# First convolution of 14 images by 2x2 minimal filtering: 16 products of 256 columns in place of 18 matmuls of 512

## The chip, the core and the metric

The kernel runs on one core of a Trainium2 chip. TensorE (PE) does matmuls into PSUM, VectorE (DVE) and ScalarE (ACT) do elementwise work, and the engines run beside each other, each through its own queue in order. The metric is the device time of one execution in microseconds, as a median of several.

## The reference, cut to what matters

Attention over 16 images of 128 channels and 32 x 32 pixels (4 heads, 1024 positions), then two 3x3 convolutions on quantised data:

```python
x = attention(x)                     # 4 heads, softmax over 1024 keys, residual
out = act_quant(x)                   # 16 levels: integers 0..15
out = conv3x3(out, weight_quant(w1)) # integers -7..7
out = batchnorm(out); out = act_quant(out)
out = conv3x3(out, weight_quant(w2))
out = batchnorm(out) + x
```

Activations and weights of the first convolution are small integers, so bf16 products summed in fp32 are exact.

## The kernel before

Attention is spread over steps: each head has 8 steps of one score group (`pss`, two fp32 matmuls, four records in the trace), one exponential on ScalarE (`e`) and one group of products with the values (`psa`). Other work is placed at fixed steps between them and shares two PSUM buffers, the pool `ps_m`: projections of queries (`psu`) and values (`psv`), and the first convolution of the image before.

```python
vp  = pool("vo", NCH + 4)            # NCH = 8: 12 value tiles
smp = pool("small", 4)
ps_m = pool("ps_m", 2, space=PSUM)
...
def project_v(b, j):
    ps = ps_m.tile([P, NH * P], F32, tag="mm", ...)
    nc.tensor.matmul(ps, lhsT=xt[b][:, ts(j, P)], rhs=bt_sb..., ...)
    vos[b, j] = vp.tile([P, NH * P], F32, tag="vo", ...)
    nc.vector.tensor_copy(vos[b, j], ps)
...
def conv(pool, tag, b, n, r, rows=RPH, group=None):
    ps = pool.tile([P, rows, W], F32, tag=tag, ...)
    for tap in range(NTAP):          # 9 matmuls of 512 columns per half image
        nc.tensor.matmul(ps, lhsT=wq[n][:, tap, :],
                         rhs=pads[b % NPAD][:, r + dy : r + dy + rows, dx : dx + W], ...)
    nc.scalar.copy(ys[b][:, r * W : (r + rows) * W], ps)
...
end = (b + 1) * NH * NCH + 2
at(end + 4, quantize, b, xt, A_LEVELS, 0.0)
for hf in range(NHF):
    at(end + 7 + hf, first_conv, b, hf * RPH)
at(end + 10, statistics, b, 0)
...
if j in (3, 4) and g + 1 < len(heads): project_u(g + 1, j - 3)
if j in (5, 6) and b + 1 < B:          project_v(b + 1, 2 * h + j - 5)
```

A scheduler fixes the order of each engine's instructions when the kernel is built (the static order). It may move work away from the step that asked for it.

## Time and profile before

| | before |
|---|---|
| time | 2154.43 us (median of 3, 2154.38 to 2155.27) |
| PE busy | 98% of the span |
| VectorE / ScalarE busy | 58% / 32% |

A group's line gives its busy time and the mean duration of one instruction. These are rows of the kernel before, each shape on its own (columns: line, engine, operation, out<-in, shapes, count, then busy us and mean ns, then idle before):

```profile
L275 PE MATMUL psc<-pad,wq 128*128 128x512 bf16 x558 | 127.9, 383 | 0.6 <-DVE pad L250 0.6
L283 ACT COPY y<-psc 128x512 f32<-128x512 f32 x62 | 36.2, 584 | 58.1 <-PE psc L275 57.5
```

The mean of 383 ns is a length with the pipeline in it. 558 matmuls in 127.9 us of busy time are 229 ns each. TensorE idled 0.6 us in all before these matmuls.

### The profile page before, as it was taken

What the parts mean: (1) busy time and instruction counts of PE and PEld (TensorE: products, weight loads), DVE (VectorE), ACT (ScalarE), POOL (GpSimd) and SP (SyncE); (2) the same over time, 40 slices, a digit from 0 to 9 for tenths busy, and PEclk for the clock granted to TensorE, in tenths of its full rate; (3) what the DMA queues carried; (4) which work ended last, traced back from release to release, by engine and by line L of the source; (5) the groups of instructions that cost most, each with busy time, mean ns of one, the idle gap of its engine ahead of it and who ended that gap; (6) DMA issues with size and microseconds to landing.
All of it is one profiled execution on the core that took longest, in us unless ns stands there. A gap on an engine that the chain in (4) does not pass through costs nothing.

```text
span 2154.1 us, 14436 instructions
## 1 busy us (share of the span) xinstructions
PE 2118.2 (98%) x5293; PEld 947.3 (44%) x5294; DVE 1256.5 (58%) x1791; ACT 695.3 (32%) x764; POOL 6.8 (0%) x16
## 2 busy tenths in 40 slices
PE   9999999999999999999999999999999999999994
PEld 4444444444444444444444444444444444444541
DVE  3665565556456565556646555665655655665676
ACT  2233232333233333333323323333332333323355
POOL 0000000000000000000000000000000000000000
PEclk9999999999999999999999999999999999999997
DMA  1000000000000000000000000000000000000043
GB/s 60 11 20 0 0 20 0 20 0 10 10 0 20 0 20 0 0 20 0 20 0 20 0 0 20 0 20 0 18 3 0 20 0 10 1 0 10 0 166 157
DMA packets 10606, 36.79 MB, mean 17 GB/s; under 512 B 1440, under 2 KB 1568, under 8 KB 10528
## 3 DMA queue, kind: packets, MB, share of 16 engines
q1 hardware_dynamic: 9872, 33.76, 4.2%
q10 hardware_dynamic: 656, 2.03, 0.3%
q8 instruction: 43, 0.70, 0.1%
q14 instruction: 35, 0.29, 0.0%
HBM read 19.01 MB, written 16.78 MB: 17 GB/s over the span
## 4 chain that ended last, share of the span: by engine, by line
PE 98%; DVE 1%; DMA 0%; ACT 0%; issue 0%; ACTq 0%; DVEq 0%
PE pss L480 41%; PE psa L504 40%; PE psc L275 6%; PE psv L459 5%; PE psu L448 5%; PE psa L619 1%; DVE y L777 1%; DMA wvo_sb<-in_wvo_dram 0%; ACT y L776 0%; DVE late L285 0%; PE ps_b L420 0%; ACT y L283 0%; DVEq L963 0%; PE ps_a L412 0%; ACTq L386 0%
## 5 line engine op out<-in xcount | busy, mean ns | idle before, releaser
L480 PE MATMUL pss<-u,x 128*128 128x512 f32 (+1 forms) x2064 | 962.4, 589 | 0.0
L504 PE MATMUL psa<-e,vo 128*128 128x512 f32 x2016 | 947.6, 592 | 0.0
L493 ACT ACTIVATE e<-pss 128x1024 f32<-128x1024 f32 x511 | 522.9, 1023 | 1305.3 <-PE pss L480 1269.2
L515 DVE TENSOR_TENSOR es<-es,e 128x1024 f32<-128x1024 f32 x378 | 461.3, 1220 | 475.3 <-ACT e L493 471.5
L480 PEld LDWEIGHTS pss<-u,x 128*128 128x128 f32 x2064 | 392.1, 190 | 487.2 <-issue 467.8
L504 PEld LDWEIGHTS psa<-e,vo 128*128 128x128 f32 x2016 | 382.6, 190 | 471.4 <-issue 466.4
L467 DVE COPY vo<-psv 128x512 f32<-128x512 f32 x128 | 88.2, 689 | 259.7 <-PE psv L459 259.7
L275 PE MATMUL psc<-pad,wq 128*128 128x512 bf16 (+3 forms) x585 | 132.0, 380 | 0.6 <-DVE pad L250 0.6
L448 PE MATMUL psu<-x,at_sb 128*128 128x512 f32 x256 | 131.1, 594 | 0.2 <-DVE at_sb L414 0.2
L459 PE MATMUL psv<-bt_sb,x 128*128 128x512 f32 x256 | 130.4, 592 | 0.0
L453 DVE TENSOR_SCALAR u<-psu,au_sb 128x512 f32<-128x512 f32 x64 | 47.9, 749 | 87.2 <-PE psu L448 87.2
L275 PEld LDWEIGHTS <-wq 128*128 128x128 bf16 x585 | 56.7, 97 | 79.9 <-issue 15.3
L527 DVE TRANSPOSE_TENSOR_REDUCE part<-es 128x32 f32<-128x1024 f32 (+1 forms) x66 | 80.6, 1221 | 2.2
L562 DVE STREAM_TRANSPOSE rb<-sums 128x1024 f32<-128x1024 f32 (+1 forms) x66 | 80.1, 1213 | 2.3
L513 DVE TENSOR_TENSOR es<-e,e 128x1024 f32<-128x1024 f32 x63 | 76.6, 1216 | 0.0
L448 PEld LDWEIGHTS psu<-x,at_sb 128*128 128x128 f32 x256 | 48.8, 191 | 61.3 <-issue 60.5
L459 PEld LDWEIGHTS psv<-bt_sb,x 128*128 128x128 f32 x256 | 48.6, 190 | 61.2 <-issue 61.2
L573 DVE TENSOR_TENSOR av<-av,rb 128x1024 f32<-128x1024 f32 x47 | 57.6, 1226 | 3.3
L574 DVE TENSOR_TENSOR acc<-acc,av 128x1024 f32<-128x1024 f32 x47 | 57.4, 1221 | 1.0
L283 ACT COPY y<-psc 128x512 f32<-128x512 f32 (+2 forms) x65 | 37.5, 578 | 59.2 <-PE psc L275 58.7
L520 ACT COPY av<-psa 128x512 f32<-128x512 f32 x63 | 36.9, 586 | 44.6 <-PE psa L504 44.6
L553 DVE COPY side<-part 32x32 f32<-32x32 f32 x252 | 43.0, 171 | 4.7
(98 smaller groups left out, 467.2 us busy)
## 6 DMA issues: line engine op xcount, KB each, us to landing
x_dram<-x SPq DMA_DIRECT2D x16, 512.0 KB, 2.6
res<-x_dram SPq DMA_DIRECT2D x16, 512.0 KB, 9.9
x<-in_x_dram SPq DMA_DIRECT2D x15, 512.0 KB, 3.6
out_dram<-y SPq DMA_DIRECT2D x15, 512.0 KB, 4.7
raw<-in_cw_dram ACTq DMA_DIRECT2D x2, 576.0 KB, 3.7
wvo_sb<-in_wvo_dram ACTq DMA_DIRECT2D x1, 514.0 KB, 7.8
out_dram<-y SPq DMA_DIRECT2D x2, 256.0 KB, 2.0
wqk_sb<-in_wqk_dram SPq DMA_DIRECT2D x1, 385.5 KB, 7.0
```

The source lines that it names most:

```text
L275: last = nc.tensor.matmul(ps, lhsT=wq[n][:, tap, :], rhs=pads[b % NPAD][:, r + dy : r + dy + rows, dx : dx + W], start=(tap == 0), stop=(t ...
L448: nc.tensor.matmul(ps, lhsT=at_sb[:, h, :], rhs=xt[b][:, ts(hf, HALF)], start=True, stop=True)
L459: nc.tensor.matmul(ps, lhsT=xt[b][:, ts(j, P)], rhs=bt_sb.rearrange("p h o -> p (h o)"), start=True, stop=True,)
L467: nc.vector.tensor_copy(vos[b, j], ps)
L480: last = nc.tensor.matmul(ps[:, ts(m, N // len(parts))], lhsT=xt[b][:, ts(key, P)], rhs=us[g][:, queries], start=True, stop=True,)
L493: exps[:] = [nc.scalar.activation(e, ps, AF.Exp).ins]
L504: nc.tensor.matmul(psa[g][m], lhsT=vos[b, j][:, ts(h, P)], rhs=e[:, ts(m, HALF)], start=(j == 0), stop=(j == NCH - 1),)
L513: nc.vector.tensor_tensor(es[g], es.pop((g, 0)), es.pop((g, 1)), ALU.add)
L515: added = nc.vector.tensor_tensor(es[g], es[g], es.pop((g, j)), ALU.add)
L527: nc.vector.tensor_reduce(part, total.rearrange("p (k c) -> p k c", c=Q), AX.X, ALU.add, apply_transpose=True,)
L562: nc.vector.transpose(rb, rinv.unsqueeze(2).to_broadcast([P, n, Q]))
L573: nc.vector.tensor_tensor(av, av, rb, ALU.mult)
```

## The change

It computes the first convolution of images 0 to 13 in 2x2 output tiles. A 4x4 piece of input is transformed (differences and sums of rows, then of columns), multiplied by transformed weights in 16 places, and the 16 results are added and subtracted into four outputs. Instead of 18 matmuls of 512 columns there are 16 of 256. The values stay exact: half and quarter integers in bf16. The transforms go to VectorE, which has room on average.

```diff
+        def transform_rows(b, part):       # 4 ops of 544 elements per image, bf16
+                nc.vector.tensor_tensor(rows[b][:, k], pick(x), pick(y), op)
+        def transform_columns(b, l):       # 4 ops of 1024, operands with step 2
+            nc.vector.tensor_tensor(tiles[b][:, l % 2], pick(x), pick(y), op)
+        def products(b, l):
+            m = qtp.tile([P, 4, D, D], F32, tag="qt", ...)
+            for k in (0, 2):
+                ps = ps_m.tile([P, 2, D, D], F32, tag="mm", ...)
+                for i in range(2):
+                    nc.tensor.matmul(ps[:, i], lhsT=wino[:, l, k + i, :],
+                                     rhs=tiles[b][:, l % 2, k + i], start=True, stop=True)
+                nc.scalar.copy(m[:, k : k + 2], ps)
+            nc.vector.tensor_tensor(e, m[:, 0:2], m[:, 2:3].to_broadcast(...), ALU.add)
+            nc.vector.tensor_tensor(into[0], e[:, 0], m[:, 3], ALU.add)
+            nc.vector.tensor_tensor(into[1], e[:, 1], m[:, 3], ALU.subtract)
+            if l >= 2: ...                 # two more ops of 512 into y
...
-                for hf in range(NHF):
-                    at(end + 7 + hf, first_conv, b, hf * RPH)
-                at(end + 10, statistics, b, 0)
+                for i in range(2):
+                    at(end + 5 + i, transform_rows, b, i)
+                    at(end + 7 + i, transform_columns, b, i)
+                    at(end + 14 + i, products, b, i)
+                    at(end + 17 + i, transform_columns, b, 2 + i)
+                    at(end + 22 + i, products, b, 2 + i)
+                at(end + 26, statistics, b, 0)
```

Cut: the one-time weight transform, and tags that let tiles share memory.

More of the change, by code (lines that the diff above doesn't have):

```diff
@@ L377, in load @@
             nc.sync.dma_start(out=xt[b], in_=x[b])
-        wqk_sb = once.tile([P, NH, 2 * P + 1], F32, name="wqk_sb")
-        wvo_sb = once.tile([P, NH, 2 * P + 1], F32, name="wvo_sb")
+        wqk_sb = once.tile([P, NH, 2 * P + 1], F32, tag="rows", name="wqk_sb")
+        wvo_sb = once.tile([P, NH, 2 * P + 1], F32, tag="tiles", name="wvo_sb")
         xt[0] = xp.tile([P, N], F32, tag="x", name="x0")
@@ L628, in attend_group @@
             if j + 1 == FIRST_STEP[i + 1] and not final:
-                avs[i] = avp.tile([P, HALF], F32, tag="avh", name=f"av_{LAST}_{i}")[:, 0:n]
+                avs[i] = avp.tile([P, N], F32, tag="av", name=f"av_{LAST}_{i}")[:, 0:n]
                 nc.scalar.copy(avs[i], psa[LAST, i])
@@ L658, in fast_path, with sums_and_differences @@
             at((n + 1) * NCH, lambda n: conv_weights(n, once, exps[0]), n)
+        wino = once.tile([P, 4, 4, P], BF16, name="wino")
+        D = W // 2
+        def sums_and_differences(out, src):
+            nc.vector.tensor_copy(out[:, 0], src[:, 0])
+            nc.vector.tensor_copy(out[:, 1], src[:, 2])
+            nc.vector.tensor_tensor(out[:, 3], src[:, 0], src[:, 2], ALU.add)
+            nc.vector.tensor_tensor(out[:, 2], out[:, 3], src[:, 1], ALU.add)
+            nc.vector.tensor_tensor(out[:, 3], out[:, 3], src[:, 1], ALU.subtract)
+            nc.vector.tensor_scalar(out[:, 2:4], out[:, 2:4], 0.5, None, ALU.mult)
@@ new lines, in transform_weights @@
+        def transform_weights():
+            with tc.issue_after(sums_added[0]):
+                by_row = once.tile([P, 4, 3, P], BF16, tag="rows", name="wino_rows")
+                sums_and_differences(by_row, wq[0].rearrange("p (y x) o -> p y x o", x=3))
+                sums_and_differences(wino, by_row.rearrange("p y x o -> p x y o"))
+        rows, tiles = {}, {}
+        OF_FOUR = (
+            (0, 2, ALU.subtract),
+            (3, 1, ALU.subtract),
+            (1, 2, ALU.add),
+            (2, 1, ALU.subtract),
+        )
@@ new lines, in transform_rows @@
+        def transform_rows(b, part):
+            pad = pads[b % NPAD]
+            if part == 0:
+                rows[b] = once.tile([P, 4, D, W + 2], BF16, tag="rows", name=f"rows_{b}")
+            pick = lambda r: pad[:, r : r + 2 * D - 1 : 2, :]
+            for k in (2 * part, 2 * part + 1):
+                x, y, op = OF_FOUR[k]
+                nc.vector.tensor_tensor(rows[b][:, k], pick(x), pick(y), op)
+        def transform_columns(b, l):
+            if l % 2 == 0:
+                tiles[b] = once.tile([P, 2, 4, D, D], BF16, tag="tiles", name=f"tiles_{b}_{l}")
+            pick = lambda c: rows[b][:, :, :, c : c + 2 * D - 1 : 2]
+            x, y, op = OF_FOUR[l]
+            nc.vector.tensor_tensor(tiles[b][:, l % 2], pick(x), pick(y), op)
@@ new lines, in products @@
+        def products(b, l):
+            m = qtp.tile([P, 4, D, D], F32, tag="qt", name=f"wino_{b}_{l}")
+            for k in (0, 2):
+                ps = ps_m.tile([P, 2, D, D], F32, tag="mm", name=f"psw_{b}_{l}_{k}")
+                for i in range(2):
+                    nc.tensor.matmul(
+                        ps[:, i],
+                        lhsT=wino[:, l, k + i, :],
+                        rhs=tiles[b][:, l % 2, k + i],
+                        start=True,
+                        stop=True,
+                    )
+                nc.scalar.copy(m[:, k : k + 2], ps)
+            y = ys[b].rearrange("p (i r j c) -> p r i j c", r=2, j=D, c=2)
+            e = once.tile([P, 2, D, D], F32, tag="raw", name=f"winoe_{b}_{l}")
+            nc.vector.tensor_tensor(
+                e, m[:, 0:2], m[:, 2:3].to_broadcast([P, 2, D, D]), ALU.add
+            )
+            into = [y[:, r, :, :, l] for r in range(2)] if l < 2 else [e[:, r] for r in range(2)]
+            nc.vector.tensor_tensor(into[0], e[:, 0], m[:, 3], ALU.add)
+            nc.vector.tensor_tensor(into[1], e[:, 1], m[:, 3], ALU.subtract)
+            if l >= 2:
+                for c in range(2):
+                    op = ALU.subtract if (l, c) == (3, 1) else ALU.add
+                    nc.vector.tensor_tensor(y[..., c], y[..., c], e, op)
@@ L690, in fast_path @@
         at(NCH + 4, lambda: constants(cleared.ins, sums_added[0]))
+        at(NCH + 6, transform_weights)
         at(2 * NCH + 4, late_bn_constants)
```

## The prediction

> **What bounds the kernel now.** I read the page's busy shares first, then the chain that ended last, then the timeline of two stretches: one with a first convolution, one where the change puts its second pair of product groups.
>
> ```profile
> PE 2118.2 (98%) x5293; PEld 947.3 (44%) x5294; DVE 1256.5 (58%) x1791; ACT 695.3 (32%) x764; POOL 6.8 (0%) x16
> ...
> PE 98%; DVE 1%; DMA 0%; ACT 0%; issue 0%; ACTq 0%; DVEq 0%
> ```
>
> TensorE is busy 98% of the span and the chain is 98% PE. Nothing else ever makes it wait for long, so a microsecond taken from its queue is a microsecond of the end, as long as no new wait appears in that queue. The other engines have room on average: VectorE 58%, ScalarE 32%.
>
> The timeline shows how dense it is, around the first convolution of image 14, whose halves are like those of the 14 images that change:
>
> ```profile
> 1836.69 2.15 PE L275 MATMUL psc<-pad,wq 128*128 128x512 bf16 x9
> ...
> 1838.67 1.88 PE L504 MATMUL psa<-e,vo 128*128 128x512 f32 x4
> ...
> 1840.39 1.88 PE L480 MATMUL pss<-u,x 128*128 128x512 f32 x4
> ```
>
> Starts are what to read (a duration contains the pipeline's length). Nine convolution matmuls take 1838.67 - 1836.69 = 1.98 us, 0.220 each. Four fp32 records take 1.72 us, 0.43 each. So one first convolution costs 2 x 1.98 = 3.96 us of TensorE, and 14 of them 55.4 us, 2.6% of the span.
>
> The price of a 256-column product is in the tail, where one piece of a convolution has 8 rows of 32:
>
> ```profile
> 2052.07 0.58 ACT L283 COPY y<-psc 128x512 f32<-128x512 f32 x1 [1.40 <-PE psc L275]
> ...
> 2053.07 0.37 ACT L283 COPY y<-psc 128x256 f32<-128x256 f32 x1 [0.42 <-PE psc L275]
> ```
>
> Each copy starts when its nine matmuls are done, so nine 256-column ones with their nine weight loads took 2053.07 - 2052.07 = 1.00 us, 0.111 each.
>
> The last stretch is head 3 of an image, from its third score step on. The change wants its second half of products there:
>
> ```profile
> 245.81 1.88 PE L480 MATMUL pss<-u,x 128*128 128x512 f32 x4
> 247.52 1.88 PE L504 MATMUL psa<-e,vo 128*128 128x512 f32 x4
> ```
>
> ```profile
> 246.28 1.22 DVE L574 TENSOR_TENSOR acc<-acc,av 128x1024 f32<-128x1024 f32 x1
> 247.42 0.68 DVE L467 COPY vo<-psv 128x512 f32<-128x512 f32 x1
> 248.02 1.22 DVE L513 TENSOR_TENSOR es<-e,e 128x1024 f32<-128x1024 f32 x1
> 249.34 1.22 DVE L515 TENSOR_TENSOR es<-es,e 128x1024 f32<-128x1024 f32 x1
> 250.48 0.68 DVE L467 COPY vo<-psv 128x512 f32<-128x512 f32 x1
> ```
>
> The two value projections of head 2 ended near 229 and 234, yet VectorE copies them out only at 247.42 and 250.48. They wait because the pool of value tiles (12: eight of this image, four of the next) has no free slot until head 3 has used its first tile, and then VectorE finishes a normalisation. All that time they hold both PSUM buffers of the small pool, the one the products need. In the kernel before nobody asks for these buffers until the projection at 250.96, so the hold is free.
>
> **What the Trainium skill says.** "TensorE: Matmul & The Clock Gate", section "Back-to-back issue gap", gives N/2.4 + 2.5 ns, 109 ns at 256 columns and 216 at 512; the trace has 111 and 220, so it agrees within 2%. The same page, section "The mechanism" of its Part 3, says weight loads overlap matmuls in flight only if they are for other row groups. The trace disagrees: 947.3 us of full-array loads lie under a PE that is 98% busy. "PSUM — Partial Sum Buffer", section "Engine vs sequencer instructions", says matmuls start and complete in program order. The trace agrees (I saw no record out of order), which means that one product that waits holds up everything behind it. "VectorE: DVE Perf Modes", section "What auto-detection actually checks", allows a two-source op its doubled rate only if every operand is 16-bit with step 1. The row transform fits that, the column transform (step 2) does not. The trace before has no bf16 two-source op, so I price all of them at the fp32 rate.
>
> **The change, part by part.**
>
> Removed from TensorE: 18 x 0.220 = 3.96 us per image. Added: 16 x 0.111 = 1.78 us. The operands are contiguous, so this may come out at 0.109. Could the fp32 weight load (190 ns) that follows a 0.11 us product stick out? In the tail's single records, fp32 loads between 8-column matmuls start 0.110 and 0.112 us apart, so it can keep up with a 256-column product; I count nothing. Net gain if nothing waits: 2.18 us per image, 30.5 us in all.
>
> Added to VectorE per image, from fp32 two-source rows (0.42 us for 256 elements, 0.68 for 512, 1.22 for 1024, so by interpolation 0.72 for 544): 4 row ops 2.9, 4 column ops 4.9, 4 sums of 512 2.7, 8 of 256 3.4, 4 into y 2.7: 16.6 us, some 232 us in all, plus about 8 us once for the weights. VectorE goes from 1256 to about 1495 us, 70%. ScalarE makes 8 copies of 0.58 us instead of 2: +3.5 us per image, +49 us. Both lie beside TensorE. The placement decides whether they stay there.
>
> So I followed the new static order of the engines with the durations of the trace. First half (groups l = 0, 1, steps 0 and 1 of head 2): both small PSUM buffers are free. ScalarE copies four pieces between exponentials (step 3.43 us, exponential 1.02, two copies 1.17, av copy 0.59: fits). VectorE's normalisation ends some 3 us later than now, but the copy that frees the attention accumulator stays ahead of the products' sums. Four exponential buffers allow a lag of about three steps; VectorE has caught up two or three steps later. No wait.
>
> Second half (head 3): the order puts the first two products of l = 2 right behind the third score step, and they wait for VectorE. In the trace's times the scores end at 247.52 and the vo copy that frees the buffer ends at 248.10; with the 0.06 us from VectorE to PE seen at the second convolution's start, the product starts at 248.16: PE waits 0.64 us. The next pair, behind one attention step, needs ScalarE's copy of the first, done near 249.4: no wait. The third needs the copy of the second: ready about 251.18, wanted at 251.20. The fourth needs the vo copy that ends at 251.16: in time. So one wait of 0.64 us per image, 9.0 us in all.
>
> Sum: 14 x (3.96 - 1.78 - 0.64) = 14 x 1.54 = 21.6 us; 2154.4 - 21.6 = 2132.8. The order of all three engines from head 60 on is the same in both kernels, so the tail gives nothing and costs nothing. I leave 2133.
>
> **Rivals.**
>
> A: no new wait counts. The full 30.5 us come, 2124. For it: the engines have room on average. Against: the held buffers are in the trace, and the queue is in order.
>
> B: VectorE becomes the local bound. Per head its work is about 18 us of 31, but from step 7 to step 2 of the next head it is nearly full already (a normalisation chain of about 7.5 us and three sums of 1.2 in 10.3 us). If the strided ops cost half again as much as priced, the lag passes from head 2 into head 3, the vo copies come later, and the wait grows to 2 us or more: the gain is gone, 2150 to 2160. Against: I count over 8 us of VectorE idle between the two halves.
>
> C: ScalarE's four copies in a row at head 3. The third and fourth products have a margin of 0.02 to 0.3 us. Copies that start 0.2 us later would cost another 0.1 to 0.4 us per image: 2135 to 2138.
>
> D: switching between fp32 and short bf16 groups (five groups per image) costs about 0.1 us each: 7 us, 2140.
>
> **Range and chances.** The sure part is 30.5 us of matmul time. The least sure is the wait, 0.64 us x 14 by my count; C and D each add up to 7 us, B more. Most errors I can see make it slower than 2133, and A bounds the other side. I take 2123 to 2146. Faster by over 2% needs 2111, which even A doesn't reach: 0.01. Slower by over 2% needs 2198, a wait of 5 us per image: 0.02. Within 2%: 0.97.
>
> **What would show it.** The products' 256-column matmuls should start 0.109 to 0.112 us apart inside a group. PE should show one idle stretch of about 0.6 us in head 3 of each of 14 images, ahead of the first l = 2 product, ended by VectorE's vo copy, 8 to 10 us in all. The period of an image should fall from 127.57 us (convolution to convolution in the chain, as 306.05 to 433.62) to about 126.0. VectorE busy should be 1450 to 1500, ScalarE about 745. I am wrong in the step "one wait" if PE idles elsewhere (before scores, on exponentials or accumulators), and in the step on weight loads if the fp32 matmul behind a group starts more than 0.13 us after the last product.

## The result

The changed kernel took 2132.52 us (median of 4, 2132.12 to 2134.57), against 2154.41 for the kernel before. The ratio is 0.9899, with a 95% interval of 0.9884 to 0.9914. The prediction was 2133.

Busy shares and the last chain of the changed kernel, by engine:

```profile
PE 2089.5 (98%) x5265; PEld 938.9 (44%) x5266; DVE 1445.9 (68%) x2139; ACT 735.7 (35%) x848; POOL 6.8 (0%) x16
...
PE 91%; DVE 7%; ACT 1%; issue 0%; DMA 0%; ACTq 0%; DVEq 0%
```

TensorE is still the bound, but the chain is no longer PE alone: 7% of it runs through VectorE. That is the sign of a wait that is on the path. The view of waits of TensorE says which (columns: who waits, on whom, us in total, times, longest; `psw` is the PSUM tile of the products):

```profile
PE psw L711 <- DVE vo L467: 6.6, 14, 0.5
```

There are 14 waits, one per image, ended by the copy of a value projection. They look smaller than they are, because the view counts from the modelled end of the last matmul. Read from start to start, the product comes 1.06 us after the last score record ahead of it, where 0.43 is usual: 0.63 us late. Summed over the single records that is 8.87 us for the 14. The timeline of TensorE in head 3 of the last changed image shows one of them:

```profile
1878.08 1.88 PE L504 MATMUL psa<-e,vo 128*128 128x512 f32 x4
1879.79 1.88 PE L480 MATMUL pss<-u,x 128*128 128x512 f32 x4
1882.13 0.38 PE L711 MATMUL psw<-tiles,wino 128*128 128x256 bf16 x2 [0.46 <-DVE vo L467]
1882.35 1.88 PE L504 MATMUL psa<-e,vo 128*128 128x512 f32 x4
1884.07 0.38 PE L711 MATMUL psw<-tiles,wino 128*128 128x256 bf16 x2
1884.29 1.02 PE L480 MATMUL pss<-u,x 128*128 128x512 f32 x2
1885.15 0.60 PE L711 MATMUL psw<-tiles,wino 128*128 128x256 bf16 x4
```

and VectorE at the same time:

```profile
1880.26 1.23 DVE L574 TENSOR_TENSOR acc<-acc,av 128x1024 f32<-128x1024 f32 x1
1881.40 0.68 DVE L467 COPY vo<-psv 128x512 f32<-128x512 f32 x1
1882.00 1.22 DVE L513 TENSOR_TENSOR es<-e,e 128x1024 f32<-128x1024 f32 x1
```

The scores free TensorE at 1879.79 + 1.72 = 1881.51, the copy ends at 1881.40 + 0.68 = 1882.08, and the product starts at 1882.13. Every other start follows without a gap. Two products take 0.22 us (1882.13 to 1882.35, 1884.07 to 1884.29), also where fp32 matmuls follow, and the last four begin 0.86 us after the two score records ahead of them, which is just what those take.

The trace shows that two things make this wait. The copy needs a value tile, and the one that it gets comes free when the products of head 3's first step end, at 1878.08 + 1.88 = 1879.96. By then VectorE has reached the end of its normalisation, and the static order puts the add into `acc` (1880.26, 1.23 us) ahead of the copy. Had the copy stood before that add, it would by my estimate have ended near 1880.26 + 0.68 = 1880.94, before the scores free TensorE. So the missing tile alone would not make TensorE wait; the add ahead of the copy does the rest. No run changed that order.

The rows of the new work in the changed kernel:

```profile
L703 DVE TENSOR_TENSOR tiles<-rows 128x1024 bf16<-128x1024 bf16 x56 | 67.1, 1219 | 0.5
L718 ACT COPY wino<-psw 128x512 f32<-128x512 f32 x112 | 61.3, 589 | 24.9 <-PE psw L711 24.9
L696 DVE TENSOR_TENSOR rows<-pad 128x544 bf16<-128x544 bf16 x56 | 22.1, 436 | 0.5
```

The column ops with step 2 take as long as fp32 ones (1219 ns for 1024 elements, against 1220 for the fp32 sums `es`). The row ops, packed, take 436 ns for 544, well under the 0.72 us priced. Both agree with what the prediction took from the Trainium skill ("VectorE: DVE Perf Modes", section "What auto-detection actually checks"), that a two-source op gets the doubled rate only if all its operands are 16-bit with step 1.

### The profile page after: what moved, and what is told of

It is laid out like the page before. It is cut to its first block, busy times and chain, and to the rows that moved or that the text cites. A ratio compares the mean times of both kernels' runs of the same rounds, so it can differ in the third digit from the quotient of the medians.

```text
span 2130.7 us, 14771 instructions
## 1 busy us (share of the span) xinstructions
PE 2089.5 (98%) x5265; PEld 938.9 (44%) x5266; DVE 1445.9 (68%) x2139; ACT 735.7 (35%) x848; POOL 6.8 (0%) x16
## 4 chain that ended last, share of the span: by engine, by line
PE 91%; DVE 7%; ACT 1%; issue 0%; DMA 0%; ACTq 0%; DVEq 0%
PE pss L480 38%; PE psa L504 37%; PE psv L459 5%; PE psu L448 5%; PE psc L275 3%; PE psw L711 1%; DVE rb L562 1%; DVE part L527 1%; DVE av L573 1%; DVE es L515 1%; DVE acc L574 1%; ACT e L493 1%; PE psa L619 1%; DVE y L856 1%; DVE side L553 0%; DVE vo L467 0%
## 5 line engine op out<-in xcount | busy, mean ns | idle before, releaser
L515 DVE TENSOR_TENSOR es<-es,e 128x1024 f32<-128x1024 f32 x378 | 461.2, 1220 | 366.4 <-ACT e L493 364.3
L275 PE MATMUL psc<-pad,wq 128*128 128x512 bf16 (+3 forms) x333 | 71.9, 377 | 0.6 <-DVE pad L250 0.6
L718 ACT COPY wino<-psw 128x512 f32<-128x512 f32 x112 | 61.3, 589 | 24.9 <-PE psw L711 24.9
L703 DVE TENSOR_TENSOR tiles<-rows 128x1024 bf16<-128x1024 bf16 x56 | 67.1, 1219 | 0.5
L574 DVE TENSOR_TENSOR acc<-acc,av 128x1024 f32<-128x1024 f32 x47 | 57.3, 1220 | 0.5
L275 PEld LDWEIGHTS <-wq 128*128 128x128 bf16 x333 | 32.2, 97 | 39.9 <-DVE pad L250 1.1
```

Source lines behind the costliest of these rows:

```text
L275: last = nc.tensor.matmul(ps, lhsT=wq[n][:, tap, :], rhs=pads[b % NPAD][:, r + dy : r + dy + rows, dx : dx + W], start=(tap == 0), stop=(t ...
L515: added = nc.vector.tensor_tensor(es[g], es[g], es.pop((g, j)), ALU.add)
L574: nc.vector.tensor_tensor(accs[b], accs[b], av, ALU.add)
```

## The experiments

The prediction came out, so the question is whether it came out for its reasons. My theory has three parts. Each product costs its place in TensorE's queue and nothing more. VectorE's added work is free. The one loss is the wait on a PSUM buffer that a value projection holds because it has no free value tile. The main rival for the last two parts is that VectorE, 189 us busier, is simply late in head 3. All kernels below but the last gave correct results.

### One value tile more

```diff
-        vp = pool("vo", NCH + 4)
+        vp = pool("vo", NCH + 5)
-        smp = pool("small", 4)
+        smp = pool("small", 2)
```

The second line only makes room.

> The change with 13 value tiles instead of 12 (and two instead of four buffers of the small pool, to make room). Theory (the wait in head 3 exists because the value projection has no free tile and so holds a PSUM buffer): the one projection is copied out at once, the order moves the second half of the products up to steps 0 and 1 of head 3, and the 14 waits of 0.63 us (8.9 us) are gone: 2123 to 2125 us, PE idle ahead of the products under 1 us in all. Rival (VectorE's extra work makes the wait, not the tile): the wait stays or comes back elsewhere, 2130 to 2133 us.

Measured: 2123.11 us (median of 4, 2121.68 to 2123.56), ratio to before 0.9852 (0.9836 to 0.9868). The first value projection of head 2 is now copied out at once (at 1855.16 in the trace), and the static order has moved the second half of the products up to steps 0 and 1 of head 3, as expected. TensorE there, in the last changed image:

```profile
1866.34 1.88 PE L504 MATMUL psa<-e,vo 128*128 128x512 f32 x4
1868.05 0.38 PE L711 MATMUL psw<-tiles,wino 128*128 128x256 bf16 x2
1868.27 1.88 PE L480 MATMUL pss<-u,x 128*128 128x512 f32 x4
1869.99 0.38 PE L711 MATMUL psw<-tiles,wino 128*128 128x256 bf16 x2
```

All gaps are the lengths of the work itself. The view of TensorE's waits has no product in it any more, and the chain that ended last is TensorE's again:

```profile
PE 98%; DVE 1%; DMA 0%; ACT 0%; issue 0%; ACTq 0%; DVEq 0%
```

The theory's 2123 to 2125 held and the rival's 2130 to 2133 did not: VectorE does the same work here (1441.2 us busy). The run changes two things at once, the tile and with it the place of the products, so it doesn't tell them apart; the next two runs keep the tiles and change the place alone.

### The second half of the products three steps later

```diff
-                    at(end + 22 + i, products, b, 2 + i)
-                at(end + 26, statistics, b, 0)
+                    at(end + 25 + i, products, b, 2 + i)
+                at(end + 29, statistics, b, 0)
```

> The change with its second half of products asked for three steps later (steps 3 and 4 of head 3), nothing else. Theory: the value copies are done by then, so the wait on them is gone: 2123.5 us if no other wait takes its place. In the static order the fourth pair of products stands half an attention step behind the third and needs a copy that shares ScalarE with an exponential and a u copy, so a new wait of up to 0.4 us per image is possible: up to 2129 us. Rival (VectorE is behind in all of head 3): no gain, 2132 us.

Measured: 2123.17 us (2123.01 to 2124.49), ratio 0.9856 (0.9839 to 0.9872). TensorE's waits name no product, and the chain has the same shares as in the run above; the feared wait on ScalarE did not come. The two cures, more tiles or a later place, end at the same time, as they should if they remove the same wait. This one changes no pool, so the smaller pool of the run above plays no part.

### The same place in the kernel before

```diff
                 for hf in range(NHF):
-                    at(end + 7 + hf, first_conv, b, hf * RPH)
-                at(end + 10, statistics, b, 0)
+                    at(end + (7, 22)[hf], first_conv, b, hf * RPH)
+                at(end + 26, statistics, b, 0)
```

> The kernel before, with the second half of each first convolution (nine matmuls of 512 columns) asked for at the place where the change asks for its second half of products. No new VectorE work, no small products. Theory (the held PSUM buffers make the wait): the same wait of 0.6 us per image appears, ended by the value copy: 2154.4 + 9 = 2163 us. Rival (the wait comes from VectorE's transforms): 2154 to 2155 us.

Measured: 2163.32 us (2161.97 to 2166.73), ratio 1.0044 (1.0027 to 1.0060). TensorE's waits in this kernel:

```profile
PE psc L275 <- DVE vo L467: 6.6, 14, 0.5
```

It is the same wait, the same 14 times and the same 6.6 us, with no transform on VectorE (busy 58%, as before) and no small product. The time is 8.9 us longer than before. The wait belongs to the place and the held buffer, and the change's work on VectorE is not needed for it.

### The input transforms and first sums issued twice

```diff
-                nc.vector.tensor_tensor(rows[b][:, k], pick(x), pick(y), op)
+                for _ in range(2):
+                    nc.vector.tensor_tensor(rows[b][:, k], pick(x), pick(y), op)
...              # likewise the column op and the sum into e
```

> The change with each row op, column op and first sum of the transforms issued twice: 1.7 + 4.9 + 2.7 = 9.3 us more VectorE work per image, 131 us in all, VectorE near 74%. Theory (VectorE's work lies beside TensorE): within 1.5 us of the change, 2131 to 2134 us. Rival (VectorE is the local bound): the lag reaches the value copies, 14 waits of 1 us or more in addition, 2145 us or more.

Measured: 2132.01 us (2130.60 to 2132.43), with VectorE busy 1563.6 us, 73%. So 118 us more of VectorE in these places cost nothing, and its work lies beside TensorE's.

### The same work issued three times

The edit is the one above with `range(3)`.

> The change with each row op, column op and first sum of the transforms issued three times: 18.6 us more VectorE work per image, VectorE near 80% of the span. Theory: the room is in places only. By the lags I add up, the row and column ops of head 0 then push the accumulator copy at the start of head 1 behind the moment when TensorE needs it, up to 3 us per image: 2135 to 2175 us. If it stays at 2132.5 the room is larger than I count.

Measured: 2132.17 us (2131.94 to 2133.61). My expectation missed. VectorE was busy 1677.0 us, 79%, and no new wait appeared. The timeline of VectorE at the start of head 1 shows how near it was:

```profile
1810.18 1.22 DVE L515 TENSOR_TENSOR es<-es,e 128x1024 f32<-128x1024 f32 x1
1811.44 1.25 DVE L527 TRANSPOSE_TENSOR_REDUCE part<-es 128x32 f32<-128x1024 f32 x1
...
1814.14 0.61 DVE L519 COPY av<-psa 128x512 f32<-128x512 f32 x1
```

TensorE starts the products that need this accumulator at 1815.13, and the copy ended at 1814.75. The lag that I had added up was too large. One reason is in the trace: repeated independent ops follow one another every 0.35 us (rows) and 1.14 us (columns), less than their durations. So the added work came to (1677.0 - 1445.9) / 14 = 16.5 us per image and not the 18.6 expected. Whether that is all of it is open. The copy came 0.4 us before it was needed here.

### Every product issued twice

```diff
-                    nc.tensor.matmul(ps[:, i], ...)
+                    for _ in range(2):
+                        nc.tensor.matmul(ps[:, i], ...)
```

> The change with every product matmul issued twice (same weights, same operand, same result): 224 more weight loads and 256-column matmuls. Theory (a product costs its place in TensorE's queue, 0.109 us with its weight load, and nothing for the switch from fp32): 2132.5 + 24.4 = 2157 us, the wait of 0.63 us per image unchanged. Rival (part of a short group lies hidden beside the fp32 work, or the fp32 weight load behind a group sticks out by 0.1 us): the difference is clearly under 22 us, or the starts behind the groups show more than 0.11 us.

Measured: 2156.36 us (2156.12 to 2156.76), 23.8 us above the change; 224 more products are 0.106 us each by the medians. The timeline of the last changed image's second half begins:

```profile
1904.90 0.60 PE L712 MATMUL psw<-tiles,wino 128*128 128x256 bf16 x4 [0.47 <-DVE vo L467]
1905.34 1.88 PE L504 MATMUL psa<-e,vo 128*128 128x512 f32 x4
1907.06 0.60 PE L712 MATMUL psw<-tiles,wino 128*128 128x256 bf16 x4
1907.49 1.02 PE L480 MATMUL pss<-u,x 128*128 128x512 f32 x2
```

In the single records products follow one another every 0.108 to 0.110 us inside a group, and whatever stands behind a group (scores or value products) starts 0.108 to 0.110 us after the last product. So no price shows for the switch back to fp32, and a product lies in the queue at full length. The 14 waits stayed at 6.6 us. The products added here cost about as much as the whole change gains (ratio to before 1.0009, 0.9992 to 1.0025).

### Without the output transform

```diff
-            y = ys[b].rearrange(...)       # e, into, and the sums into y
-            ...
+            if l == 3:
+                nc.vector.tensor_copy(ys[b]..., m...)
```

The result is wrong (relative error 0.93).

> The change without the output transform (wrong result on purpose: y is one plain copy of the last group's products per image): some 9 us less VectorE work per image, among it everything that VectorE does with the products between the two halves. Theory (the wait is set by the value tile and the normalisation ahead of its copy): the wait stays, 2131.5 to 2133.5 us. Rival (the transforms make VectorE late for the value copy): the wait shrinks, 2124 to 2129 us.

Measured: 2132.90 us (2132.35 to 2133.65), VectorE 1351.3 us, 63% (6.8 us less per image, where 9 were expected). The wait stayed at 6.5 us in the view. Taking about 95 us from VectorE gained nothing, as giving it 231 us more cost nothing.

## Why the prediction was right

- **Matmul time.** Predicted 3.96 - 1.78 = 2.18 us per image; measured 3.96 - 16 x 0.109 = 2.22. The prediction held 0.109 possible because the operands are contiguous; that this is the reason was not tested. The doubled products show the price by itself.
- **One wait.** Predicted 0.64 us in head 3, ahead of the first l = 2 product, ended by the vo copy, and no other; measured 8.87/14 = 0.63 in just that place. Its cause is a value projection that still holds the buffer when the product wants it. That is shown from three sides: one more tile removes the wait, a later place removes it, and the same place in the kernel before creates it. The prediction also named the second half of the cause, that VectorE "finishes a normalisation" before the copy; that half is read from the timeline and not shown by a run.
- **The sum.** 14 x (3.96 - 1.74 - 0.63) = 22.3 us; measured 21.9 by the medians. The period of an image, from its first product to the next image's, is 125.98 to 126.00 us in 12 of 13 cases, against 127.57 before and about 126.0 predicted.
- **Rivals.** A (no wait) said 2124 and was 8.5 us too low; one more tile brings it about. B (VectorE the local bound) is refuted for the amount of its work by the doubled, tripled and removed transforms; the order of its work still sets when the wait ends. C (ScalarE's copies late) and D (a price for switching) do not appear: all starts behind those places are on time.
- **What was off.** VectorE was predicted at 1450 to 1500 us and came out at 1445.9. Of the 49 us between 1495 and that, 16 are the row ops: 4 x 0.72 = 2.9 us per image priced, 4 x 0.436 = 1.7 measured. The larger part is that I added durations of ops that overlap at their ends: in the single records the durations grow by 221 us in sum, the busy time by 189. ScalarE was predicted at about 745 and measured 735.7, for the second reason alone (49.5 us more in durations, 40.4 in busy time). Neither is on the path, so neither moved the time.

The version with 13 value tiles is faster than both kernels: 2123.11 us, 1.5% under the kernel before.

## What to carry to other kernels

When the bound engine's queue is full, the gain of a change is the time it takes out of that queue minus the new waits in it, and here both came out of starts in the trace before and the new static order. Before placing work at a step, ask who holds the buffers it needs at that step, also when the holding costs nothing today: a buffer that waits 18 us for its copy is harmless only until somebody else wants it. A wait on VectorE was here no proof that VectorE was too busy: work added to it elsewhere, or taken away, left the wait as it was. Then look at what stands ahead of the late instruction in its queue.

## What the Trainium skill lacked or had wrong

- "TensorE: Matmul & The Clock Gate", section "The mechanism": one of its points lets weight loads overlap matmuls in flight only for other row groups, and the prediction quotes that. The opening of the same section also allows a load into the background weight buffer. The trace contradicts the point, and doesn't show which buffer is loaded: full-array loads of 938.9 us lie beside a TensorE that is 98% busy, and matmuls with a new weight each follow every 0.109 us.
- The same page, section "Back-to-back issue gap": it gives about 131 ns per matmul of 512 columns as the sustained rate in a stream with weight loads, and calls N/2.4 + 2.5 too high there. The prediction used the formula and left this out. In this kernel the formula holds in such a stream (0.109 us at 256 columns; at 512 the commonest steps in the single records of the kernel before are 0.215 and 0.216, 245 of 529), and none is under 0.214.
- The same page, section "LDWEIGHTS (loading the stationary operand)": P/1.2 is 107 ns at 128 columns and has no type in it; that fp32 is slower can only be guessed from the table on fast weight load that follows. The trace has 95 to 98 ns for bf16 and 190 for fp32. Yet in the kernel before fp32 loads between short matmuls start 0.110 to 0.112 us apart, so the recorded length is not the interval at which loads can follow.
- "Perfetto Trace Analysis", section "Optimization Strategy", says that a gap that repeats can mean too little SBUF or PSUM for the next tile. It lacks that the short pool need not be the one whose tile is waited for: here a product waited for PSUM, because a copy held it that waited for a tile of another pool and then stood behind an add. It cost 8.87 us.
